# Half-height transposes and crossed projections in two places of four, with the rounding of silu's rows carried into the next step

## The chip, the cores and the metric

The kernel runs as one program on one core of a Trainium2 chip. The metric is the device time of one execution in microseconds, the median of several. Engines are named as in the profile: PE is TensorE's matmul, PEld its weight load, DVE is VectorE, ACT is ScalarE, POOL is GpSimd, SP is SyncE, which only issues DMAs here. SBUF is the on-chip memory with 128 partitions, PSUM the accumulator memory of eight banks into which PE writes.

## The reference

For each of 16 sequences of 512 rows and 256 columns, `x` is normalised to `xn`, and the result is `x + s * silu(ffn(xn))`. Two branches are computed from `xn`:

```python
# branch one: s, attention with a kernel over positions, then a feed-forward block
v = xn @ v_w + v_b                                     # 16 heads of 16
kern = einsum(weights of the 8 best of 16, sum of sines)   # one value per distance, per head
causal_kern = 3 * step(kern) * window
scores = causal_kern[i - j] + qm[i] + km[j] + 0.15 * (qc @ kc.T) / sqrt(8)
attn = softmax(where(i >= j, scores, -1e9))
h = layernorm(xn + (attn @ v) @ out_w + out_b)
s = layernorm(h + gelu(h @ ffn_w1 + b1) @ ffn_w2 + b2)

# branch two: a gated block whose inputs and weights are rounded to FP4 in blocks of 16 columns
def fp4_quant_dequant(x):
    scale = maximum(max(abs(block)) / 6, 1e-12)
    return nearest of (0, .5, 1, 1.5, 2, 3, 4, 6) to abs(x / scale), * sign * scale
hid = silu(q(xn) @ q(w_gate).T) * (q(xn) @ q(w_up).T)  # 704 columns
g = silu(q(hid) @ q(w_down).T)
out = x + s * g
```

All matrices are float32.

## The kernel before

The program keeps all weights in SBUF and goes through the 16 batches in order, each in four steps, here called places 0 to 3. A step works on four attention heads over all 512 rows, and at the same time on 128 rows of branch two (place t handles rows 128t to 128t+127). Work of three batches overlaps: while the heads of batch b are computed, the output, layer norm and feed-forward of batch b-1 (`old`) run in the same steps, and the projection of batch b+1 or b+2 is prepared. PE, DVE and ACT execute their instructions in exactly the order in which the main loop (lines 1149 to 1256) writes them; POOL and SP too run in program order.

One step runs so:

1. `context` (line 514): the products `cp` of the previous step's attention weights with the values, accumulated in one PSUM bank of its own, `cp`. `kept` (528) copies it to SBUF as `ct`, with columns reversed.
2. Five bursts of scores. Each burst has a `ws` group on PE, its Exp on ACT (`weights`, 478) and a multiplication by a table of the position kernel on POOL (`tabled`, L512 in the profile), and an `ms` group on PE, which computes scores of the next step for their row maxima, taken by DVE (`junk`, `mx`; `maxima`, 439).
3. Between the bursts other work is placed by the strings of `PLAN` (748), one for each place: `W` a `ws` burst, `M` an `ms` burst, `!` the maxima of what was found, and other letters one piece of a generator: `c` a piece of the next projection (`project`, 309), `l` a piece of the old batch's attention output (`output`, 550), `f` a piece of the old feed-forward's second product (`contract`), `x` the transposes of the rounded input of branch two (`turned_x`, 678), `y` those of silu's rounded rows (`turned_hidden`, 720, tiles `hqtp`), `h` those of the normalised rows, `k` a `kept` held back.
4. `hidden` (692): gate and up products of branch two in two halves of 352 columns. The first half goes to two ring banks (`gp`, `up`), the second to a pair of banks shared with the scores (`gu`). Between the halves PE turns the maxima (`mp`).
5. `gate` (730): the down product `dp` of the rows of the previous step, from the transposes of step 3.
6. In places 1 and 2, `expand` (616): the first product of the old batch's feed-forward with its Gelu, half of the rows in each. Places 0 and 3 have pieces of projections here.
7. The rounding of this step's 704 columns, `fp4_stages` (196): DVE takes the maximum of each block (`amax`) and its inverse, POOL multiplies by it (L222). Two DVE tensor_scalar passes make `m`, a power of two from the exponent bits times a constant; adding `m` and subtracting it rounds. POOL multiplies by the block's scale (L232). `ROUNDING` (670) gives the add and the subtraction to DVE, except in place 3, where POOL subtracts (L231). All of it is written before the next step begins.

`output` handles two row tiles of 128 at a time. For each, four groups of heads are transposed (`ctp`), divided by their softmax sums on DVE (`rinv`, `cx`), transposed back (`ct2`, shown as `ct<-ident,cx`), copied by ACT (`cT`), and multiplied by `wo` on top of a bias product (`op`). A helper `by_halves` (293) already does some transposes in halves of 64 rows, which go to the two banks of one pair: place 2 and 3's `xqtp` and one `htp`.

PSUM holds a pair used by `ws` and the second half of `hidden`, the bank of `cp`, and a ring of five banks for all else. Input rows `x` of batch b+2 are loaded and normalised at place 3 of batch b, and transposed (`xtp`) in place 0 of the next; the rounded input of branch two for rows 256 to 511 of a batch is made in its own place 1.

Quoted: the places' plans before.

```python
PLAN = ("WMc!llWM!xWM!ccllyWMlyW!M!l", "WMll!kWM!lWM!xllyhWMccy!WM!l",
        "WM!fffxM!fWffM!ffhM!ffWffM!fWfffWyy", "WM!fffxM!fWffM!ffWfM!ffWffM!fWffyy")
```

Of the kernel before, what the change touches and what calls it, by code (L numbers as in the profile page):

```python
# [13 lines left out]
I32 = mybir.dt.int32  # L14
# [30 lines left out]
LEVEL = 6291456.0  # L45
EXPONENT = 0x7F800000
# [4 lines left out]
def tile_block(ctx: ExitStack, tc: tile.TileContext, a: dict, pos: bass.AP, win: bass.AP, out: bass.AP):  # L51
# [45 lines left out]
    ps_c = ctx.enter_context(tc.tile_pool(name="ps_c", bufs=1, space=PSUM))  # L97
    ps = ctx.enter_context(tc.tile_pool(name="ps", bufs=5, space=PSUM))
# [95 lines left out]
    v_aug = [keep.tile([P, NT, H, VS], F32, name=f"va{i}", tag=f"va{i}") for i in range(2)]  # L194

    def fp4_stages(dst, src, n, width, engines=(dve, dve)):
# [26 lines left out]
        nc.gpsimd.tensor_scalar(scale, amax, 1.0 / 6.0, 1e-12, ALU.mult, ALU.max)  # L223
        yield
        m = sb.tile([P, I_FF], F32, name="m", tag="m")[:n, :width]
        dve.tensor_scalar(m.bitcast(I32), dst.bitcast(I32), EXPONENT, None, ALU.bitwise_and)
        dve.tensor_scalar(m, m, 1.0, LEVEL, ALU.max, ALU.mult)
        yield
        engines[0].tensor_tensor(dst, dst, m, ALU.add)
        yield  # L230
        engines[1].tensor_tensor(dst, dst, m, ALU.subtract)  # L231
        nc.gpsimd.tensor_tensor(blocks(dst), blocks(dst), per_block(scale), ALU.mult)  # L232

    def fp4(dst, src, n, width):
        for _ in fp4_stages(dst, src, n, width):
            pass
# [19 lines left out]
    mask = sb.tile([P, S], F32, name="mask", tag="mask")  # L256
# [14 lines left out]
    cp = ps_c.tile([P, S], F32, name="cp", tag="cp")  # L271
# [21 lines left out]
    def by_halves(name, dst, blocks):  # L293

        acc = ps_s.tile([P, 2, S], F32, name=name, tag="ws")
        for i, src in enumerate(blocks):
            for upper in range(2):
                k = slice(64 * upper, 64 * upper + 64)
                turn(acc[:, upper, i * 64 : (i + 1) * 64], src[k, :], ident[k, k])
        n = len(blocks) * 64  # L300
        act.copy(
            dst.rearrange("p (i u t) -> p u i t", u=2, t=64), acc[:, :, :n].rearrange("p u (i t) -> p u i t", t=64)
        )
# [4 lines left out]

    def project(b, x):

        xns[b] = []
        for pair in range(2):
            xns[b].append(sb.tile([P, 2, D], F32, name=f"xn_{b}_{pair}", tag="xn", bufs=6))
            for t in (2 * pair, 2 * pair + 1):
                act.activation(
                    rows_of(xns[b], t), x[:, t, :D], AF.Identity, bias=nmr[b][:, t : t + 1], scale=rstd[b][:, t : t + 1]
                )
            yield 0.0
# [64 lines left out]
        acc = projected(wq, P)  # L383
        split(acc, *halves("q", "hT" if b > 1 else "lo"), True, MIX / math.sqrt(8.0), None, (content(qi, 0, 1), content(qi, 2, 3)))
        yield 1.71
        acc = projected(wk, P)
        split(acc, *halves("k", "lo"), False, 1.0, None, (content(ki, 0, 2), content(ki, 1, 3)))
        yield 1.71
# [12 lines left out]
        va = v_aug[b % 2]  # L401
        vas[b] = va
        for t in range(NT):
# [3 lines left out]
            act.copy(va[:, t, :, 0:HD], vp[:, :D].rearrange("p (h d) -> p h d", d=HD))  # L407
# [106 lines left out]
    def context(b, g, where):  # L514

        for j in range(NT):
            n = S - j * P
            for i in range(4):
                mm(
                    cp[SLOT * i : SLOT * i + VS, :n],  # L520
                    vas[b][:, j, 4 * g + i, :],
# [4 lines left out]
                )  # L526

    def kept(b, g):
# [21 lines left out]
    def output(b, h, cts, half, mv):  # L550

        cTs, ops = {}, []

        def normal(t):
            tp = bank(f"ctp_{b}_{t}").rearrange("p (h s) -> p h s", s=SLOT)
            for g in range(H // 4):
                turn(tp[:, 4 * g : 4 * g + 4, :].rearrange("p h s -> p (h s)"), cts[g][:, t * P : (t + 1) * P])
            rinv = sb.tile([P, H], F32, name=f"rinv_{b}_{t}", tag="rinv", bufs=2)
            dve.reciprocal(rinv, tp[:, :, HD])
            cx = sb.tile([P, H, HD], F32, name=f"cx_{b}_{t}", tag="cx", bufs=3)  # L560
            dve.tensor_tensor(cx, tp[:, :, 0:HD], rinv.unsqueeze(2).to_broadcast([P, H, HD]), ALU.mult)
            return cx.rearrange("p h d -> p (h d)")

        def turned(t, cx):
            t2 = bank(f"ct2_{b}_{t}")
            for c in range(NC):
                turn(t2[:, c * P : (c + 1) * P], cx[:, c * P : (c + 1) * P])
            cTs[t] = sb.tile([P, D], F32, name=f"cT_{b}_{t}", tag="cx", bufs=3)
            act.copy(cTs[t], t2[:, :D])

        def product(t):
            acc = bank(f"op_{b}_{t}")
            op = acc[:, :D]
            biased(acc, 0, 1)
            cT = cTs[t]
            for c in range(NC):
                mm(op, cT[:, c * P : (c + 1) * P], wo[:, c, :], start=False, stop=(c == NC - 1), skip_group_check=True)
            later.append(lambda: added(h, (t,), acc, mv))

        first, second = 2 * half, 2 * half + 1  # L580
        cx = normal(first)
        yield 0.43
        cx2 = normal(second)
        yield 0.43
        turned(first, cx)
        yield 0.21
        turned(second, cx2)
        yield 0.21
        product(first)
        yield 0.96  # L590
        product(second)
        yield 0.96
# [23 lines left out]
    def expand(b, half, hT):  # L616

        acts = []
        for f in range(NF):
# [4 lines left out]
            act.activation(acts[f], fp[:, : 2 * P], AF.Gelu, bias=fb1[:, f : f + 1])  # L624
        return acts
# [44 lines left out]
    ROUNDING = [[dve if e == "d" else nc.gpsimd for e in by] for by in ("dd", "dd", "dd", "dg")]  # L670

# [20 lines left out]
    def hidden(b, t, xqT):  # L692
# [3 lines left out]
        def halves():  # L696
            for s in range(2):
                cut = slice(s * HI, (s + 1) * HI)
                if s == 1:
# [18 lines left out]
        return hid, halves(), fp4_stages(hid[:, :I_FF], hid[:, :I_FF], P, I_FF, ROUNDING[t])  # L718
# [18 lines left out]
    def expect(function):  # L737
# [6 lines left out]
        ("dddr|crd|dcdypr|xcr|cydd", "prrppo"),  # L744
        ("r|px|rpp|p|yyr", "pp"),
        ("p|x||yytt|tt", ""),
    )
    PLAN = ("WMc!llWM!xWM!ccllyWMlyW!M!l", "WMll!kWM!lWM!xllyhWMccy!WM!l", "WM!fffxM!fWffM!ffhM!ffWffM!fWfffWyy", "WM!fffxM!fWffM!ffWfM!ffWffM!fWffyy")

    def keeping(b, g):  # L750
        kept(b, g)
        yield 0.0

    def turning_h(b, half):
        turned_hs[half] = turned_h(b, xns[b], half, half == 1)
        yield 0.43

# [21 lines left out]
    plain = sb.tile([1, 2, D], F32, name="plain", tag="plain")  # L779
# [3 lines left out]
    nc.scalar.dma_start(out=vb, in_=a["v_b"].rearrange("(c p) -> p c", p=P))  # L783
# [247 lines left out]
    for k in range(H // 2 + 2):  # L1031
# [20 lines left out]
        if k > 1:  # L1052
            i = k - 2
            row = 2 * M * (i % 4)
# [9 lines left out]
    dve.memset(cp, 0.0)  # L1064
# [43 lines left out]
    nc.sync.dma_start(out=wo, in_=a["out_w"].rearrange("(c p) n -> p c n", p=P))  # L1108
# [32 lines left out]
    waiting, hq, cts, turned_hs, acts, coming, mv = None, None, [], {}, {}, None, None  # L1141
    xqTs, hqTs = {}, {}
# [6 lines left out]
    for s in range(STEPS):  # L1149
# [5 lines left out]
        if waiting is not None:  # L1155
            context(*waiting)
            if g != 1 or not has_old:
                kept(*waiting[:2])
# [176 lines left out]
```

## Time and profile before

| what | us |
|---|---|
| median of three runs (1848.93, 1850.88, 1851.63) | 1850.88 |
| profiled execution, its own time | 1850.01 |
| its span in the profile | 1848.3 |
| one batch in the steady part, four steps (756.17 to 860.00) | 103.83 |
| PE busy in that batch | 102.01 |
| DVE, ACT, POOL busy in that batch | 87.39, 62.31, 78.08 |
| one product by the table on POOL, mean of 448 | 1.75 |

The profile is that of one execution. A group of instructions in it stands under the line that recorded it; most engines' instructions were recorded by one helper at L72, so groups are told apart by the names of their tiles, as `hqtp<-ident,wide`. In a list over time a row has its start, its length, the engine, the line, the operation, out<-in, the partitions by elements and how many instructions were joined (x7); brackets at the end give the engine's idle time ahead of the row and what ended it. In a list of windows each engine has its busy time in that stretch. The length of a PE row includes the pipeline's fill, so that the distance of two starts, not the length, is what a group costs on PE. An expression like `PEclk` 1.00 is the share of full clock that TensorE was granted.

### The profile page before, as it was taken

Reading aid. Unit: us, or ns where it says so; the run is one execution under the profiler, and the core shown is the slowest. Engines: PE = TensorE matmul, PEld = TensorE weight load, DVE = VectorE, ACT = ScalarE, POOL = GpSimd, SP = SyncE. Lnnn points to the kernel's source line nnn. Section 1 sums busy time; section 2 is a strip of 40 time slices with the busy share of each in tenths; the row PEclk is TensorE's granted clock in tenths of the full one; section 3 lists DMA queues with packets and bytes.
Section 4 is the critical chain, followed back from the end, with each engine's and each line's share of the span. In section 5 each row is a group of like instructions: output and inputs, shape, how many; then the busy total and the mean of one; then the engine's idle time right before and its main releaser. Section 6 shows DMA issues by size and latency. Waiting matters only on the chain.

```text
span 1848.3 us, 33981 instructions
## 1 busy us (share of the span) xinstructions
PE 1745.7 (94%) x11491; PEld 1247.9 (68%) x11491; DVE 1487.9 (81%) x3917; ACT 1068.6 (58%) x1823; POOL 1313.4 (71%) x1128
## 2 busy tenths in 40 slices
PE   5769799999999999999999999999999999999998
PEld 2235467676776767677776767677776767677677
DVE  4868688888888888788888878888888888888754
ACT  5644455656565565556565565556566665555553
POOL 5467576778687776778687776778677776778671
PEclk8869799999999999999999999999999999999999
DMA  6254142423334242323334242323334242323200
GB/s 202 88 161 128 62 145 82 137 62 103 110 98 129 62 136 82 119 74 108 111 98 129 62 134 84 110 82 105 114 96 121 69 135 86 92 88 94 66 22 12
DMA packets 127122, 184.82 MB, mean 100 GB/s; under 512 B 15315, under 2 KB 57749, under 8 KB 126949
## 3 DMA queue, kind: packets, MB, share of 16 engines
q1 hardware_dynamic: 122496, 181.25, 31.8%
q8 instruction: 91, 1.49, 0.3%
q10 hardware_dynamic: 4004, 0.98, 0.3%
q14 instruction: 83, 0.67, 0.1%
q0 software_dynamic: 448, 0.42, 0.1%
HBM read 136.45 MB, written 45.09 MB: 98 GB/s over the span
## 4 chain that ended last, share of the span: by engine, by line
PE 76%; DVE 11%; POOL 3%; issue 1%; ACT 0%; DVEq 0%; POOLq 0%
PE f L72 23%; PE dp L72 8%; PE gu L72 7%; PE cp L72 7%; DVE junk L72 5%; PE ws L72 4%; PE op L72 4%; PE gp L72 4%; PE up L72 4%; PE ms L72 4%; PE vp L72 3%; PE hqtp L72 2%; POOL pr L512 2%; DVE cx L72 1%; PE qk_wk L72 1%; PE qk_wq L72 1%
## 5 line engine op out<-in xcount | busy, mean ns | idle before, releaser
L512 POOL TENSOR_TENSOR pr<-pr,table 128x1024 f32<-128x1024 f32 (+2 forms) x448 | 767.8, 1748 | 73.7 <-ACT pr L72 72.9
L72 DVE CUSTOM_DVE_ANT_0 junk<-ms,mask 128x512 bf16<-128x512 f32 (+3 forms) x1024 | 502.0, 490 | 148.3 <-PE ms L72 69.1
L72 ACT ACTIVATE pr<-ws 128x1024 f32<-128x1024 f32 x320 | 328.4, 1026 | 131.3 <-PE ws L72 126.4
L72 PE MATMUL f<-w,act 64*128 64x256 f32 (+1 forms) x1984 | 282.2, 382 | 0.0
L72 ACT ACT_TABLE_LOAD x168 | 215.5, 1283 | 64.1 <-PE gp L72 48.6
L72 PE MATMUL f<-hT,w 128*128 128x256 f32 x1024 | 226.3, 379 | 0.0
L72 PEld LDWEIGHTS f<-hT,w 128*128 128x128 f32 x1024 | 194.5, 190 | 26.6 <-ACT hT L72 0.2
L72 PEld LDWEIGHTS f<-w,act 64*128 64x128 f32 (+1 forms) x1984 | 197.8, 186 | 13.7
L232 POOL TENSOR_TENSOR wide<-wide,scale 128x704 f32<-128x704 f32 (+1 forms) x71 | 96.6, 1360 | 145.7 <-DVE wide L72 144.4
L72 PE MATMUL ws<-qT,kT 38*128 38x512 f32 (+3 forms) x1024 | 170.6, 388 | 21.3 <-ACT pr L72 16.4
L72 PE MATMUL ms<-kT,qT 36*128 36x512 f32 (+3 forms) x1024 | 166.2, 356 | 11.4 <-DMA kT<-k_d 6.7
L72 PE MATMUL dp<-wdT,hqT 128*128 128x256 f32 x768 | 176.2, 379 | 0.0
L72 PEld LDWEIGHTS dp<-wdT,hqT 128*128 128x128 f32 x768 | 145.8, 190 | 31.4 <-issue 6.7
L72 ACT ACTIVATE act<-f,fb 128x256 f32<-128x256 f32 x256 | 118.2, 474 | 75.3 <-PE f L72 72.4
L72 PE MATMUL cp<-pr,va 128*17 128x512 f32 (+3 forms) x2048 | 151.5, 434 | 0.0
L72 PEld LDWEIGHTS ws<-qT,kT 38*128 38x128 f32 x1024 | 90.4, 188 | 76.8 <-ACT pr L72 36.3
L223 POOL TENSOR_SCALAR scale<-amax 128x32 f32<-128x32 f32 (+1 forms) x104 | 39.2, 376 | 116.0 <-DVE amax L72 112.9
L72 PEld LDWEIGHTS cp<-pr,va 128*17 128x17 f32 x2048 | 54.3, 97 | 99.4 <-issue 75.3
L72 PEld LDWEIGHTS ms<-kT,qT 36*128 36x128 f32 x1024 | 104.7, 190 | 21.4 <-issue 14.4
L72 DVE TENSOR_TENSOR wide<-wide,m 128x704 f32<-128x704 f32 (+2 forms) x126 | 112.1, 889 | 4.1
L222 POOL TENSOR_TENSOR wide<-wide,inv 128x704 f32<-128x704 f32 (+1 forms) x71 | 99.1, 1396 | 21.6 <-DVE inv L72 21.1
L72 DVE SCALAR_TENSOR_TENSOR xn<-xn,rs,b 128x256 f32<-128x256 f32 x124 | 79.8, 643 | 35.9 <-POOL rs L114 30.7
(217 smaller groups left out, 3109.7 us busy)
## 6 DMA issues: line engine op xcount, KB each, us to landing
table<-rv SPq DMA_DIRECT2D x64, 1024.0 KB
kT<-k_d SPq DMA_DIRECT2D x256, 76.0 KB
qT<-q_d SPq DMA_DIRECT2D x256, 72.0 KB
x<-in_L_attn_x_dram SPq DMA_DIRECT2D x21, 512.0 KB
q_d<-q_hi SPq DMA_DIRECT2D x32, 256.0 KB
q_d<-q_lo SPq DMA_DIRECT2D x32, 256.0 KB
k_d<-k_hi SPq DMA_DIRECT2D x32, 256.0 KB
k_d<-k_lo SPq DMA_DIRECT2D x32, 256.0 KB
```

The costliest lines, as they stand in the source:

```text
L72: return lambda *args, **kw: self.follow(op(*args, **kw))
L222: nc.gpsimd.tensor_tensor(blocks(dst), blocks(src), per_block(inv), ALU.mult)
L223: nc.gpsimd.tensor_scalar(scale, amax, 1.0 / 6.0, 1e-12, ALU.mult, ALU.max)
L232: nc.gpsimd.tensor_tensor(blocks(dst), blocks(dst), per_block(scale), ALU.mult)
L512: nc.gpsimd.tensor_tensor(part, part, table[:, mine, j * P :], ALU.mult)
```

## The change

- `output` makes its transposes in halves of 64 rows, in two banks: eight half transposes for two row tiles in each direction. The products with `wo` run as pairs of 64-row matmuls, with one bias of half height for both tiles, and are joined by the existing `added_halves`.
- `project` computes q and k, and two of the four value tiles, by `crossed`: matmuls of 64 rows that go to two banks in turns, the second phase with the halves exchanged. It runs inside the bursts of places 0 and 1; its input is transposed in place 3, a step earlier (letter `i`), with the load of `x` at place 2, `xn` in seven buffers, and the small products `qk_m` at the end of place 0.
- `cp` comes from the ring, now of six banks, with a stationary of 32 columns in place of 17.
- The rounding of silu's rows and of branch two's input: ACT's Abs times 2^22 writes `m` in bfloat16, and two DVE scalar_tensor_tensor operations take `max(m, 1.25 * 2^22)` and add and subtract it. Weights keep the old way. Place 3's subtraction returns to DVE.
- The rounding of places 3 and 0 is carried into the next step: letter `a` does Abs or the add, `z` the rest with POOL's scaling. That of places 1 and 2 runs inside `expand`.
- In places 0 and 1 `hidden` takes the pair of score banks for its first half, and the transposes `hqtp` come behind the turned maxima, between the two halves. The transposes `xqtp` are in halves there too.
- The rounded input of rows 256 to 511 of a batch is made in place 3 of the batch before.
- Rows of `wo` and `v_b` are loaded in another order to suit the halves.

```diff
-        engines[0].tensor_tensor(dst, dst, m, ALU.add)
-        yield
-        engines[1].tensor_tensor(dst, dst, m, ALU.subtract)
+        if by_act:
+            nc.gpsimd.tensor_scalar(scale, amax, -1.0 / 6.0, -1e-12, ALU.mult, ALU.min)
+            yield
+            m = sb.tile([P, I_FF], BF16, name="m", tag="m")[:n, :width]
+            act.activation(m, dst, AF.Abs, scale=POWER)
+            yield
+            dve.scalar_tensor_tensor(dst, m, 1.25 * POWER, dst, ALU.max, ALU.add)
+            yield
+            dve.scalar_tensor_tensor(dst, m, 1.25 * POWER, dst, ALU.max, ALU.subtract)
...
         nc.gpsimd.tensor_tensor(blocks(dst), blocks(dst), per_block(scale), ALU.mult)
...
+    def crossed(acc, stationary, moving):
+        for phase, c in itertools.product(range(2), range(NC)):
+            for i in range(2):
+                k = slice(64 * i, 64 * i + 64)
+                of = i ^ phase
+                mm(
+                    acc[of], stationary(of, k, c), moving(of, k, c),
+                    start=(phase == 0 and c == 0), stop=(phase == 1 and c == NC - 1), skip_group_check=True,
+                )
+            yield phase, c
...
     def output(b, h, cts, half, mv):
+        tiles = (2 * half, 2 * half + 1)
+        acc = [bank(f"ctp_{b}_{half}_{upper}") for upper in range(2)]
+        for i, (t, g) in enumerate(itertools.product(tiles, range(H // 4))):
+            for upper in range(2):
+                k = slice(64 * upper, 64 * upper + 64)
+                turn(acc[upper][:, 64 * i : 64 * (i + 1)], cts[g][k, t * P : (t + 1) * P], ident[k, k])
...
+        acc = [bank(f"op_{b}_{half}_{upper}") for upper in range(2)]
+        biased(acc[0], 0, 2, 64)
...
-                if s == 1:
+                if s == in_pair:
                     both = ps_s.tile([P, 2, S], F32, name=f"gu_{b}_{t}", tag="ws")
...
     PLAN = (
+        "WM!lM!xWacclWM!llWcM!WcMz!ll",
+        "WM!lkxM!WacclWM!llWccM!WllMz!h",
+        "WM!fffxM!fWffM!ffhM!ffWffM!fWfffWyy",
+        "WM!fffxM!fWiffM!ffWfM!iffWffM!fWffyy",
+    )
...
-        pair, more = {1: (b, 2), 2: (b + 1, 0)}.get(g), iter(())
+        pair, more = {1: (b, 2) if b == 0 else None, 2: (b + 1, 0), 3: (b + 1, 2)}.get(g), iter(())
...
-        hq, halves, stages = hidden(b, g, xqTs.pop((b, g)))
+        hq, halves, stages = hidden(b, g, xqTs.pop((b, g)), 0 if has_old and g < 2 else 1)
         before = (b, g)
         ops = ahead
         next(halves)
         if following:
             subtracted(*following, ahead)
+        if has_old and g < 2:
+            for _ in hand["y"]:
+                pass
         next(norms, None)
         next(norms, None)
         next(halves)
         next(stages)
...
-            acts[g - 1] = expand(old, g - 1, turned_hs[g - 1])
+            acts[g - 1] = expand(old, g - 1, turned_hs[g - 1], stages)
...
-        for _ in stages:
-            pass
+        if has_old and g % 3:
+            for _ in stages:
+                pass
```

## The prediction

> **What bounds the kernel now.** I read the totals of the page first, then the busy time of each engine over one batch cut at its four steps, then the timelines of POOL and PE inside a step. Totals:
>
> ```profile
> PE 1745.7 (94%) x11491; PEld 1247.9 (68%) x11491; DVE 1487.9 (81%) x3917; ACT 1068.6 (58%) x1823; POOL 1313.4 (71%) x1128
> ```
>
> PE is busy 94%, but that average hides where it is not. The busy times of one batch, cut where each `cp` begins (columns: window, its length, PE, PEld, DVE, ACT, POOL, granted clock, DMA share, GB/s):
>
> ```profile
> 756.17:780.20 24.03, 22.76 (x141) 14.72 (x140) 19.53 (x58) 14.64 (x24) 18.40 (x14) 1.00 0.37 118
> 780.20:808.72 28.52, 27.97 (x180) 20.39 (x179) 25.21 (x68) 17.88 (x31) 19.29 (x15) 1.00 0.50 152
> 808.72:836.67 27.95, 27.95 (x210) 22.25 (x209) 23.92 (x58) 16.52 (x26) 21.25 (x19) 1.00 0.18 50
> 836.67:860.00 23.33, 23.33 (x181) 17.75 (x181) 18.73 (x52) 13.28 (x21) 19.14 (x16) 1.00 0.26 85
> sum 103.83, PE 102.01 PEld 75.10 DVE 87.39 ACT 62.31 POOL 78.08; mean PE 25.50 PEld 18.78 DVE 21.85 ACT 15.58 POOL 19.52
> ```
>
> Places 2 and 3 are PE from end to end; places 0 and 1, which the change rewrites, have PE idle 1.27 and 0.55 us. So PE sets each step, and a step gets shorter only if no other engine's chain becomes its length. The nearest other chain is POOL's. The POOL timeline of the steps of place 0 and place 1:
>
> ```profile
> 760.51 1.39 POOL L232 TENSOR_TENSOR wide<-wide,scale 128x704 f32<-128x704 f32 x1
> 761.86 11.94 POOL L512 TENSOR_TENSOR pr<-pr,table 128x1024 f32<-128x1024 f32 x7
> ...
> 783.05 1.39 POOL L232 TENSOR_TENSOR wide<-wide,scale 128x704 f32<-128x704 f32 x1 [3.12 <-DVE wide L72]
> 784.39 12.12 POOL L512 TENSOR_TENSOR pr<-pr,table 128x1024 f32<-128x1024 f32 x7
> ```
>
> Seven multiplications by the table run back to back for 12 us. The last scaling of silu's rows (1.39) runs before them, and what follows, `cp`, comes at 780.20 and 808.72, 6.4 and 12.2 us after the blocks end (773.80, 796.51): today the block is no limit. PE in the step of place 1:
>
> ```profile
> 782.48 0.51 PE L72 MATMUL ws<-qT,kT 38*128 38x512 f32 x2
> ...
> 788.84 0.60 PE L72 MATMUL hqtp<-ident,wide 128*128 128x128 f32 x4
> ...
> 794.29 1.35 PE L72 MATMUL gp<-wgT,xqT 128*128 128x352 f32 x4
> ...
> 796.66 0.27 PE L72 MATMUL mp<-ident,mx 128*16 128x128 f32 x1
> ...
> 799.13 2.75 PE L72 MATMUL dp<-wdT,hqT 128*128 128x256 f32 x12
> 801.72 7.07 PE L72 MATMUL f<-hT,w 128*128 128x256 f32 x32
> ```
>
> `hqtp`, which reads the scaled rows, is at 6.4 us after the first `ws`; then gate, up, `dp`, expand and the next `cp` follow with no gap.
>
> **The change, part by part.** All numbers are for a batch from the second on, times within a step from its first `ws`.
>
> *Less on PE.* In halves of 64 rows a transpose is cheaper: the rows with 64 partitions show 8 in 0.215 us, against 0.109 each for the full ones. Twelve `ctp`/`ct2`/`xqtp` transposes a step of places 0 and 1 give 1.5 us a batch; two joined biases instead of four (0.22 each to the next start) 0.6; fewer changes between 64 and 128 rows (0.11 each, 12 to 16 fewer) 1.3 to 1.8; the projection (3.43 for q and k), the value tiles (0.86) and the products stay as long, since a pair of 64-row matmuls takes 0.436 and two passes of a full one 0.43. With 1.8 us of stalls gone PE could be 4 to 5 us a batch shorter, all in places 0 and 1. The transposes of x move to place 3 (0.93), which gives a value tile (0.96) to place 1. Places 2 and 3 stay at 27.95 and 23.3.
>
> *Rounding.* Two DVE passes (0.53 each at the row `m<-wide`, more where POOL is in the way) become one Abs on ACT. No row has an Abs of 704 elements; the ACT rows of 512 (copy 0.59) and 1024 (Exp 1.03) bound it, and I take 0.75. DVE falls by about 8 us a batch, ACT rises by 4 to 66: both stay below PE, so the sums give nothing and cost nothing. The two other passes become scalar_tensor_tensor with a maximum. Not shown at 704; the row of the same shape without the scalar, 0.91, is its price unheld. Place 3's subtraction leaves POOL (1.69) for DVE.
>
> *The late scaling: where it goes wrong.* Rows of places 3 and 0 are now rounded inside the next step's weights. In the program order of POOL the scaling of these rows comes behind the seven table products, and PE's `hqtp` waits for it. `hqtp` is moved behind `mp`, and everything after it on PE, gp and up, `dp`, expand or `qk_m`, and the next `cp`, is queued behind that wait. So POOL's chain becomes the step.
>
> Place 1: the first Exp ends at 1.58 (0.55 from `ws` to Exp, as 782.48 to 783.02, then 1.03); the block from 1.65 to about 13.7; scaling 1.39: 15.1. Behind it `hqtp` 0.71, gp and up 2.37, `dp` 2.60, expand 7.0, `cp` 2.28: 14.96. Sum 30.05, against 28.52: +1.53. PE itself would be there at 12 to 13 (gp starts at 11.8 today; less `hqtp` 0.76, stalls 0.5 and about 1 of halves; plus gate and up of the first half 2.37 and `mp` 0.11; up to 1 more for waits on the maxima in DVE).
>
> Place 0: the ct copy stands before the first Exp, which ends at 1.65; the third weights come about 0.4 late behind Abs and cT copies on ACT; block to 14.03, scaling to 15.4; `hqtp` 0.71, gp and up 2.37, `dp` 2.68, `qk_m` 0.57, `cp` 2.28: 8.61. Sum 24.0, as now. POOL alone: +1.5 a batch.
>
> *DVE and POOL in each other's way.* Two rounding passes with two inputs in SBUF now fall inside the block of place 0 and of place 1. The profile shows what such an operation does beside POOL's:
>
> ```profile
> 828.54 1.28 DVE L72 SCALAR_TENSOR_TENSOR xn<-xn,mv,g 128x256 f32<-128x256 f32 x1
> ...
> 828.30 1.23 POOL L222 TENSOR_TENSOR xq<-xn,inv 128x512 f32<-128x512 f32 x1
> 829.50 0.90 POOL L663 TENSOR_TENSOR gated<-gated,xn 128x256 f32<-128x256 f32 x1
> ...
> 831.23 0.73 POOL L663 TENSOR_TENSOR gated<-gated,xn 128x256 f32<-128x256 f32 x1
> ```
>
> The DVE operation, 0.46 when alone, ends at 829.82, 0.29 after POOL's operation (829.53): it has waited for it. The next POOL operation then takes 0.90 in place of 0.73. For 704 elements the part behind POOL's end is 0.28 x 704/256 = 0.77, less the 0.11 that POOL gets back: 0.66 for each pass, 1.3 a step, 2.7 a batch, all on the chain just made critical. Bounds: 0 (they find POOL between two operations) and 0.91 each, 3.6 a batch. I take 2.7.
>
> [...]
>
> *The clock.* PE now idles 2 to 4 us in one piece in places 0 and 1. What idling does to the clock (columns as above):
>
> ```profile
> 1719.50:1723.08 3.58, 0.00 (x1) 0.03 (x1) 3.44 (x7) 0.84 (x1) 0.58 (x1) 1.00 0.00 0
> 1723.79:1730.62 6.83, 6.79 (x27) 5.12 (x27) 4.25 (x16) 2.73 (x5) 6.83 (x5) 0.50 0.00 1
> ```
>
> After 3.58 us without PE the granted clock is 0.50 for 6.8 us. A shorter dip is in the profile too: the step of place 1 that begins at 1091.72 has 3.4 us of half clock in the middle and takes 30.04, not 28.52: 1.5 a dip. Five of the 15 such steps have it. Bounds: none, and one in each of the two steps, 3.0 a batch. A gap of 2 to 4 us against a row of 3.58 is nearer to the full end, so 2.2 a batch, less the 0.5 that these steps lose today: +1.7.
>
> [...]
>
> *The rest.* `cp` takes a ring bank and 32 columns, at the same streaming length: nothing, since `cp`'s predecessor in the bank is several products old. ct's copy and the loads of x (issued at place 2, from SP, behind which only loads of scores queue; DMA share 0.18 there) are hidden; if the cover were gone, a load of x would be late by its landing, some 2 us, once a batch. Three more DMAs at the start lie beside the loading of weights, 0 to 1 us. Without a ready batch, start and first batch: DVE has fewer passes, PE more halves: -2, bounds -6 and +2. End: -1.
>
> *Sum.* 1.5 + 2.7 + 1.7 = 5.9 a batch, 15 batches, 88; less 3 for both ends: +85. The profiled execution took 1850.01 (span 1848.3), 0.9 under the median 1850.88, so the sum needs no correction: 1850 + 85 = 1935.
>
> **Rivals.**
> A: only the late scaling costs; the passes slip between POOL's operations and the clock holds. 15 x 1.5 - 3 = +20: 1870. For it: the block's length has hardly varied (11.94, 12.12); against it: the held rows.
> B: scaling and contention, no more half clock: 15 x 4.2 - 3 = +60: 1910. For it: gaps under 3.58.
> C, the other side: `hqtp` isn't late, and PE's savings show. This needs the scaled rows by 12.7 in place 1 (13.6 is the point at which that step is as long as before) and 13.4 in place 0; POOL's 12 us of products and 1.39 would have to be 2 us shorter or the block to start before the first Exp has ended. Then place 1 is 12.65 + 14.95 = 27.6 and place 0 22.0: -2.9 a batch, 1850 - 15 x 2.9 = 1806. Durations on POOL speak against it.
> D: worse. Abs, at 0.75, stands before an Exp and leaves POOL without work for that long in both steps: another 1.5 a batch: 1958.
> E: halves are no cheaper than full transposes (the change does not do what it says on PE). As POOL sets the step it moves little: as my forecast.
>
> **From cases to numbers.** Forecast with E 0.42, B 0.22, A 0.18, D 0.08, C 0.10. Of C I give 0.02 to a time within 0.2% of before (which is what a measurement here can tell from no change) and 0.08 to faster. The forecast's own range is 1915 to 1955. The range of 8 in 10 leaves out C and the upper half of D: 1864 to 1956.
>
> **What would show it.** Right: in places 0 and 1 POOL's scaling follows the seven products, PE idles before `hqtp` with POOL as releaser for 2 us or more, steps of 24 to 26.5 and 30 to 32.5, blocks of 13 us or more in place of 12, granted clock under 1.00 in them, DVE near 80 a batch and ACT near 66. Places 2 and 3 unchanged. Wrong: `hqtp` starts without a wait, place 1 under 28.5, or the block still ends by 12; then the step that failed is the POOL order or its block's start.

## The result: 10% slower, twice the loss that was forecast

The changed kernel takes 2037.43 us (median of 2034.19 to 2041.93) against 1850.12 for the kernel before, a ratio of 1.101 with a 95% interval of 1.099 to 1.104. The forecast was 1935, 1864 to 1956: the sign was right, and the time lies 81 us above the range. The profiled execution took 2034.19, its span is 2032.5.

The totals of the page of the changed kernel:

```profile
PE 1773.7 (87%) x12383; PEld 1286.4 (63%) x12383; DVE 1408.6 (69%) x3736; ACT 1123.9 (55%) x1921; POOL 1341.5 (66%) x1112
```

PE's share falls from 94% to 87%, though its busy time is 28 us longer: there are waits, and time at half clock. Where they are, the busy times of one batch show, cut at each `cp` as for the kernel before (window, length, PE, PEld, DVE, ACT, POOL, granted clock, DMA share, GB/s):

```profile
708.31:733.51 25.20, 21.88 (x178) 14.01 (x180) 20.37 (x55) 13.75 (x22) 18.83 (x13) 1.00 0.49 152
733.51:773.21 39.70, 31.23 (x205) 23.84 (x197) 21.16 (x61) 19.33 (x34) 19.55 (x14) 0.83 0.26 78
773.21:801.08 27.87, 27.87 (x209) 21.94 (x208) 21.99 (x55) 17.50 (x28) 22.05 (x19) 1.00 0.19 56
801.08:824.32 23.24, 23.24 (x185) 17.89 (x184) 19.27 (x55) 15.26 (x25) 20.19 (x18) 1.00 0.27 92
sum 116.01, PE 104.22 PEld 77.68 DVE 82.80 ACT 65.83 POOL 80.62; mean PE 26.06 PEld 19.42 DVE 20.70 ACT 16.46 POOL 20.16
```

Places 2 and 3 are as before (27.87, 23.24), place 0 is 1.2 longer, at 25.20. Place 1 takes 39.70 in place of 28.52, with a mean clock of 0.83: there lie 11.2 of the 12.2 us that this batch is longer. Over the batches place 1 takes 37.9 to 41.2 (the last batch apart), and place 0 takes 25.2 or 26.9. PE in that step (start, length, work, idle time ahead and what ended it):

```profile
735.78 0.49 PE L73 MATMUL ws<-qT,kT 38*128 38x512 f32 x2
...
742.56 0.76 PE L73 MATMUL ms<-kT,qT 36*128 36x512 f32 x1 [4.55 <-DMA kT<-k_d]
...
755.89 0.28 PE L73 MATMUL mp<-ident,mx 128*16 128x128 f32 x1 [2.12 <-DVE mx L73]
757.59 1.54 PE L73 MATMUL hqtp<-ident,wide 128*128 128x128 f32 x6 [1.42 <-POOL wide L242]
758.92 2.55 PE L73 MATMUL gp<-wgT,xqT 128*128 128x352 f32 x4
```

The wait for POOL ahead of `hqtp` is there, as forecast. But it is not the largest. In the second burst `ms` waits 4.55 us for a DMA, a load of `kT`; the forecast doesn't name that wait. (`qT` and `kT` are the operands of the scores in SBUF; the projected q and k lie in `q_d` and `k_d` in between, and are stored there from the tiles `q_hi`, `q_lo`, `k_hi`, `k_lo` and `ml`.) What precedes this load on its queue (SP's issues from place 0 on):

```profile
719.34 0.32 SPq L466 DMA_DIRECT2D qT<-q_d  x1
719.71 0.25 SPq L467 DMA_DIRECT2D kT<-k_d  x1
...
721.00 1.22 SPq L378 DMA_DIRECT2D q_d<-q_hi  x2
722.32 1.36 SPq L378 DMA_DIRECT2D k_d<-k_hi  x2
726.16 1.16 SPq L378 DMA_DIRECT2D q_d<-q_lo  x2
727.42 1.20 SPq L378 DMA_DIRECT2D k_d<-k_lo  x2
...
731.71 0.36 SPq L466 DMA_DIRECT2D qT<-q_d  x1
732.12 0.25 SPq L467 DMA_DIRECT2D kT<-k_d  x1
734.80 1.72 SPq L393 DMA_DIRECT2D q_d<-ml  x4
736.62 1.76 SPq L393 DMA_DIRECT2D k_d<-ml  x4
738.42 0.39 SPq L466 DMA_DIRECT2D qT<-q_d  x1
738.86 0.25 SPq L467 DMA_DIRECT2D kT<-k_d  x1
```

Place 1 needs eight loads of scores operands. Two pairs are issued at 719 to 720, the first after 6.8 us of waiting for a `ws` of PE; the third and fourth pair stand behind the stores of the next batch's q and k. (In the source all eight loads are written behind these stores: the order that counts is the one that SP was given when the program was built.) The stores of `q_lo` wait for DVE, which makes it at 725.44, and the stores of `ml` for the small products `qk_m`, which the change puts at the end of place 0. So the last load is issued at 738.86, 19.5 us after the first, and PE has its data at 742.56. In the batch of the kernel before that was cut into steps above, the eight loads go out from 767.90 to 774.87, and the stores of q and k from 776.62 on:

```profile
767.90 0.32 SPq L418 DMA_DIRECT2D qT<-q_d  x1
...
774.87 0.42 SPq L419 DMA_DIRECT2D kT<-k_d  x1
776.62 1.22 SPq L350 DMA_DIRECT2D q_d<-q_hi  x2
```

### The profile page after: what moved, and what is told of

Same layout as the page of the kernel before. It is cut to its first block, busy times and chain, and to the rows that moved or that the text cites. A ratio compares the mean times of both kernels' runs of the same rounds, so it can differ in the third digit from the quotient of the medians.

```text
span 2032.5 us, 35418 instructions
## 1 busy us (share of the span) xinstructions
PE 1773.7 (87%) x12383; PEld 1286.4 (63%) x12383; DVE 1408.6 (69%) x3736; ACT 1123.9 (55%) x1921; POOL 1341.5 (66%) x1112
## 4 chain that ended last, share of the span: by engine, by line
PE 64%; POOL 10%; DVE 6%; ACT 4%; issue 3%; DMA 3%; SPq 2%; POOLq 0%; DVEq 0%; ACTq 0%
PE f L73 22%; POOL pr L560 8%; PE dp L73 7%; PE cp L73 6%; PE gp L73 4%; PE up L73 4%; PE gu L73 4%; PE ws L73 3%; PE ms L73 3%; DMA kT<-k_d 3%; PE hqtp L73 3%; PE vp L73 2%; ACT pr L73 2%; DVE wide L73 2%; SPq L393 2%
## 5 line engine op out<-in xcount | busy, mean ns | idle before, releaser
L560 POOL TENSOR_TENSOR pr<-pr,table 128x1024 f32<-128x1024 f32 (+2 forms) x448 | 806.5, 1825 | 240.4 <-ACT pr L73 236.4
L73 PE MATMUL ms<-kT,qT 36*128 36x512 f32 (+3 forms) x1024 | 198.2, 393 | 86.4 <-DMA kT<-k_d 78.3
L73 ACT ACT_TABLE_LOAD x168 | 215.5, 1283 | 46.0 <-PE gu L73 27.4
L73 DVE SCALAR_TENSOR_TENSOR wide<-m,wide 128x704 f32<-128x704 bf16 x130 | 165.0, 1270 | 108.1 <-ACT m L73 105.9
L73 PEld LDWEIGHTS f<-hT,w 128*128 128x128 f32 x1024 | 194.5, 190 | 26.7 <-ACT hT L73 0.3
L73 PE MATMUL ws<-qT,kT 38*128 38x512 f32 (+3 forms) x1024 | 187.7, 406 | 20.7 <-ACT pr L73 9.0
L73 PEld LDWEIGHTS ms<-kT,qT 36*128 36x128 f32 x1024 | 116.6, 201 | 114.7 <-issue 80.2
L73 PE MATMUL cp<-pr,va 128*32 128x512 f32 (+3 forms) x2048 | 151.9, 435 | 0.0
L73 PEld LDWEIGHTS ws<-qT,kT 38*128 38x128 f32 x1024 | 102.2, 202 | 63.9 <-ACT pr L73 24.7
L222 POOL TENSOR_TENSOR wide<-wide,inv 128x704 f32<-128x704 f32 (+1 forms) x71 | 105.6, 1487 | 25.8 <-DVE inv L73 23.4
L73 PEld LDWEIGHTS cp<-pr,va 128*32 128x32 f32 x2048 | 62.1, 110 | 89.7 <-issue 69.4
L73 PE MATMUL gp<-wgT,xqT 128*128 128x352 f32 x256 | 109.2, 559 | 0.0
```

Of the source, the lines that this page charges most:

```text
L73: return lambda *args, **kw: self.follow(op(*args, **kw))
L222: nc.gpsimd.tensor_tensor(blocks(dst), blocks(src), per_block(inv), ALU.mult)
L560: nc.gpsimd.tensor_tensor(part, part, table[:, mine, j * P :], ALU.mult)
```

## The experiments

Steps are given as place 0 / place 1 in the steady part. Places 2 and 3 keep their 27.9 and 23.2 in all runs. The changed kernel has 25.2 / 39.7.

### Stores behind the loads

```diff
             def rest():
                 dve.scalar_tensor_tensor(lo[:, step], acc, by, hi[:, step].bitcast(F32), op, ALU.subtract)
-                for half, to in zip((hi, lo), places):
-                    for place in to:
-                        nc.sync.dma_start(out=place, in_=half.bitcast(F32))
+                def store():
+                    for half, to in zip((hi, lo), places):
+                        for place in to:
+                            behind_loads(nc.sync.dma_start(out=place, in_=half.bitcast(F32)))
+                stores.append(store)
...
             ahead = operands(*divmod(s + 2, H // 4))
+        caught_up(False)
```

The small parts of q and k (`ml`) likewise. In place 0 the stores that were put aside are issued by the last line; `behind_loads` orders each of them behind the last load of `operands`.

> The changed kernel, with one thing altered: in place 0 SP issues the stores of the next batch's q and k, and of their small parts, after the loads of scores operands of that step instead of between them. Theory S (the stores stand in SP's queue ahead of a load that place 1 needs, and the stall of 4.6 us on kT, with the half clock behind it, is most of the missing time): step of place 1 falls from 39.7 us to 31.4 to 33, no PE idle time with kT as releaser, 15 x about 7 = 105 us less, 1915 to 1945. Rival P (POOL's chain alone sets places 0 and 1, the late load lies beside it): place 1 stays over 37, time over 2000.

Measured: 1942.47 us, ratio 1.0498 (1.047 to 1.0525); 95 us less. The window of place 1 and the batch's sum:

```profile
922.62:955.67 33.05, 28.58 (x205) 21.22 (x197) 21.23 (x61) 19.16 (x34) 19.53 (x14) 0.95 0.38 117
...
sum 109.36, PE 101.56 PEld 75.02 DVE 82.83 ACT 65.68 POOL 80.59; mean PE 25.39 PEld 18.76 DVE 20.71 ACT 16.42 POOL 20.15
```

25.2 / 33.05 in most batches, and no wait for `kT` in the steady part. The last load of `kT` is issued at 910.81, the first store at 911.18. Half of the loss was the order of SP's queue. With it gone the kernel is at 1942, 7 us from the forecast of 1935, which had left these stores out. The rest of the forecast can now be read term by term, POOL first:

```profile
901.44 13.56 POOL L577 TENSOR_TENSOR pr<-pr,table 128x1024 f32<-128x1024 f32 x7 [0.63 <-ACT pr L73]
914.96 1.38 POOL L242 TENSOR_TENSOR wide<-wide,scale 128x704 f32<-128x704 f32 x1
...
926.54 13.37 POOL L577 TENSOR_TENSOR pr<-pr,table 128x1024 f32<-128x1024 f32 x7 [1.57 <-ACT pr L73]
939.87 1.39 POOL L242 TENSOR_TENSOR wide<-wide,scale 128x704 f32<-128x704 f32 x1
```

and PE of the same two steps:

```profile
914.70 0.28 PE L73 MATMUL mp<-ident,mx 128*16 128x128 f32 x1 [0.69 <-DVE mx L73]
916.40 0.87 PE L73 MATMUL hqtp<-ident,wide 128*128 128x128 f32 x6 [1.42 <-POOL wide L242]
...
939.61 0.28 PE L73 MATMUL mp<-ident,mx 128*16 128x128 f32 x1 [2.25 <-DVE mx L73]
941.31 0.98 PE L73 MATMUL hqtp<-ident,wide 128*128 128x128 f32 x6 [1.42 <-POOL wide L242]
942.08 2.55 PE L73 MATMUL gp<-wgT,xqT 128*128 128x352 f32 x4
944.43 1.81 PE L73 MATMUL up<-wuT,xqT 128*128 128x352 f32 x4
```

The first `ws` of these steps starts at 899.71 and 924.89, so `hqtp` starts at 16.7 and 16.4 us. The forecast's sums, 15.4 + 1.3 in place 0 and 15.1 + 1.3 in place 1, are 16.7 and 16.4. The last three products of the block show why it is longer (kernel with the stores behind the loads, then the kernel before):

```profile
908.89 6.11 POOL L577 TENSOR_TENSOR pr<-pr,table 128x768 f32<-128x768 f32 x3
```

```profile
769.00 4.80 POOL L512 TENSOR_TENSOR pr<-pr,table 128x768 f32<-128x768 f32 x3
```

6.11 against 4.80 is 1.31 more, for two DVE passes: 0.66 each, as worked out. And `gp`, 1.35 at full clock, takes 2.55.

### Rounding of places 3 and 0 in its own step

```diff
-        if has_old and g % 3:
+        if has_old:
             for _ in stages:
                 pass
```

> The changed kernel, with the rounding of places 3 and 0 finished in its own step, as before the change; the transposes hqtp stay late, SP's order of stores stays. Theory S: the late scaling is worth 2 to 4 us a batch, the late load of kT stays with all its price: 1975 to 2010, place 1 still 36 or more. Rival P (the late scaling is the whole cost): PE no longer waits for POOL in places 0 and 1, and the time is at or under 1850.

1978.55 us, ratio 1.0691 (1.0666 to 1.0716). That is 59 us less than the changed kernel. From the second batch on PE waits for POOL in hardly any step of places 0 and 1, the wait for `kT` is still there (4.3 to 5.9 us), place 1 is at 33.7 to 35.1, under the 36 that theory S gave it. POOL's late scaling alone was not the whole cost, as theory S had it. But place 0 got no shorter: 24.2 in some batches and over 27.5 in most.

### Both alterations

> Both alterations together: stores behind the loads, and rounding of places 3 and 0 in its own step. What is left of the change are the halves, the crossed projections, Abs on ACT and cp in the ring. Theory: no wait on POOL or kT in places 0 and 1, PE sets all four steps: 22 to 23.5, 27.6 to 28.5, 27.9, 23.3; 1805 to 1850. Rival D (DVE, whose two rounding passes stand between the steps again, delays the maxima and so the bursts): places 0 and 1 as long as before or longer, 1850 to 1890.

1952.17 us, ratio 1.0557 (1.0528 to 1.0585). My theory fell and rival D held: 10 us slower than with the stores alone, at 24.2 to 30.3 / 29.1 to 32.6. In place 0, on DVE, POOL and PE:

```profile
799.52 4.54 DVE L73 SCALAR_TENSOR_TENSOR wide<-m,wide 128x704 f32<-128x704 bf16 x2 [1.14 <-ACT m L73]
```

```profile
799.47 0.73 POOL L728 TENSOR_TENSOR gated<-gated,xr 128x256 f32<-128x256 f32 x1
800.97 2.35 POOL L577 TENSOR_TENSOR pr<-pr,table 128x1024 f32<-128x1024 f32 x1 [0.76 <-ACT pr L73]
```

```profile
804.72 1.22 PE L73 MATMUL qk_wq<-xnT,wq 64*128 64x512 f32 x1 [2.47 <-DVE mx L73]
```

The two rounding passes take 4.54 here: they end 0.74 after POOL's first table product (803.32). With POOL idle (from 767.49 to 773.87) they take 1.82, as in a place 1 of the changed kernel:

```profile
771.91 1.82 DVE L73 SCALAR_TENSOR_TENSOR wide<-m,wide 128x704 f32<-128x704 bf16 x2 [5.89 <-ACT m L73]
```

Behind them on DVE stand the first maxima, so PE stops for 2.47 us in the third burst and then has half the clock (0.83 over the step). What the two passes lose by waiting for POOL, 2.72 here (4.54 less 1.82), is more than the 1.31 that POOL lost to two passes with the stores behind the loads, and my forecast had counted only the latter.

### Scaling late, passes early

With the stores behind the loads, the rounding of places 3 and 0 in its own step, and POOL's last scaling ordered behind the seventh product (the three pieces are Abs and the two passes):

```diff
+            for _ in range(3):
+                next(stages)
...
+        if by_act and tables_done:
+            tc.add_manual_dep(last.ins, tables_done[-1].ins.name, in_order, reason="scale behind the tables")
```

> Stores behind the loads; Abs and the two DVE rounding passes of places 3 and 0 in their own step, but POOL's last scaling of those rows still held behind the seven table products of the next step. It tells the two terms of my forecast apart: against the first kernel of this call it has no DVE pass with two SBUF inputs beside the table products, against the third it has the late scaling. Forecast's terms: 2.7 us a batch less than the first (40 us) plus up to 1.7 a batch of clock, and 1.5 + 2.9 = 4.4 a batch (66 us) more than the third: 1870 to 1905. Rival (contention costs nothing): equal to the first within 10 us.

1972.65 us, ratio 1.0662 (1.0634 to 1.0691), outside what I expected: 25.3 to 29.3 / 32.3. It was meant to take the contention away, but only moved it to the head of the step, as in the run before. PE again stops up to 2.5 us for the first maxima in place 0. So it doesn't separate the two terms; what it shows is that the late scaling still costs on top (20 us over the kernel with both alterations).

### More passes in the block

```diff
     def completed(pieces):
+        for _ in range(2):
+            spare = sb.tile([P, S], BF16, name="spare", tag="junk")
+            dve.scalar_tensor_tensor(spare, wgT[:, 0, :S], 1.0, wuT[:, 0, :S], ALU.max, ALU.min)
         for _ in pieces:
```

> The kernel with the stores behind the loads, and two more DVE passes with two SBUF inputs (512 wide, result unused) put ahead of the two real ones inside POOL's block of places 0 and 1: the suspected cost doubled. By the forecast's rule each adds 0.28 x 512/256 - 0.11 = 0.45 us to POOL's block, 0.9 a step: blocks 13.5 to 14.4, steps 25.2 to 26.1 and 33.05 to 34, 15 x 1.8 = 27 us more than that kernel (1942): 1960 to 1980. Rival (DVE's passes cost POOL nothing, the block was long for another reason): blocks as before, time within 8 us of that kernel.

2036.05 us, ratio 1.1005 (1.0984 to 1.1026): 94 us more than the kernel with the stores alone, not 27; steps 30.0 / 35.0. On DVE, POOL and PE:

```profile
953.79 2.33 DVE L73 SCALAR_TENSOR_TENSOR spare<-wgT,wuT 128x512 bf16<-128x512 f32 x2
956.04 3.96 DVE L73 SCALAR_TENSOR_TENSOR wide<-m,wide 128x704 f32<-128x704 bf16 x2
```

```profile
952.62 5.71 POOL L577 TENSOR_TENSOR pr<-pr,table 128x768 f32<-128x768 f32 x3
```

```profile
961.91 0.38 PE L73 MATMUL mp<-ident,mx 128*16 128x128 f32 x1 [4.17 <-DVE mx L73]
```

POOL's last three products take 5.71, that is 0.91 more than in the kernel before, 0.45 for each added pass, as the forecast's sum has it. But the whole blocks, 13.16 and 12.98, are under the 13.5 to 14.4 that were expected, and under those without the added passes (13.56, 13.37). For the first real pass now meets the last product, the longest (2.35 in the kernel before), and waits for its end (958.33): it no longer lengthens the block. The maxima come late, and `mp`, not `hqtp`, sets the step. So in this run the price on POOL is as forecast for the passes that end before the block does (0.45 each), and the larger price is on DVE, which is the later of the two: its two real passes take 3.96, against 1.82 with POOL idle.

### Useless matmuls in the idle time

```diff
+    def filling(n):
+        acc = bank("filling")
+        for i in range(n):
+            mm(acc[:, : 2 * P], wgT[:, 0, :P], wgT[:, 0, : 2 * P], start=True, stop=True)
...
         next(halves)
+        if has_old and g == 1:
+            filling(10)
         if following:
             subtracted(*following, ahead)
         if has_old and g < 2:
+            filling(6)
             for _ in hand["y"]:
```

> The kernel with the stores behind the loads, and matmuls whose result nobody reads, put into PE's idle time: 10 (2.2 us) before the maxima are turned in place 1, 6 (1.3 us) before hqtp in places 0 and 1. If the idle time itself brings the half clock after it, the step of place 1 falls from 33.05 to 31.3 to 31.6 with the clock at 1.00 and place 0 stays at 25.2: 15 x 1.6 = 24 us less than that kernel, 1910 to 1925. Rival (the half clock has another cause, or the filling delays hqtp): 1942 or more.

1969.44 us, ratio 1.0641 (1.062 to 1.0663), 26.2 / 34.2, as the rival had it: I had the size wrong, since the trace has 20 instructions for the 10 of these matmuls (4.48 us) and 12 for the 6 (2.76 us), and the filling delayed `hqtp` by 2.9 us in place 1. From `hqtp` to the next `cp` it is 12.6 us, against 14.4 without filling. With half as many:

> As the kernel with the filling matmuls, but with half as many (each counted double there and delayed hqtp by 2.9 us in place 1 and 1 us in place 0; what followed hqtp still took 12.6 us at full clock, 14.4 without filling). If the idle time brings the half clock: place 1 at 31.3 to 31.7 in place of 33.05, place 0 at 25.2, 1910 to 1925, against 1942 with the stores behind the loads alone. Rival (the shorter tail came from something else): 1940 or more.

```profile
911.79:943.16 31.37, 30.37 (x221) 23.24 (x213) 21.15 (x61) 19.14 (x34) 19.52 (x14) 1.00 0.39 123
```

1911.47 us, ratio 1.033 (1.0313 to 1.0347), 25.2 / 31.37 at full clock: 31 us less than without the useless work. `hqtp` starts 16.4 us after the first `ws`, as without filling, and what follows is shorter: here the idle time itself brings the half clock (0.95 over the step without filling, 1.00 with it), at 1.7 us a batch in place 1. In place 0 it does so in some batches: without filling four of the first 14 such steps take 26.7 to 27.2, with it all 14 take 25.2. Both together are 2.1 us a batch (31 over 15).

### hqtp last

With the stores behind the loads (and behind the maxima): in places 0 and 1 the second half of gate and up before `mp`, and then, ahead of `hqtp` and `dp`, `qk_m` in place 0 and expand in place 1.

```diff
+        if has_old and g == 1:
+            acts[g - 1] = expand(old, g - 1, turned_hs[g - 1], stages)
+        if has_old and g < 2:
+            for _ in hand["y"]:
+                pass
         if gating:
             gate(*gating, hqTs.pop(gating))
```

> The kernel with the stores behind the loads (and behind the maxima), and hqtp later still: in places 0 and 1 gate and up of the second half come first, and in place 1 the whole of expand (7 us), in place 0 the small products qk_m; only then hqtp and dp. POOL's chain is then off the path. Theory: place 0 22.8 to 23.8, place 1 27.6 to 28.6, no half clock; 102 a batch against 104.3 of the kernel before: 1810 to 1840. Rival (the maxima on DVE, late by the held passes, hold mp and so the next ws): place 1 over 29.5, no faster than before.

1887.36 us, ratio 1.0199 (1.0172 to 1.0225), 23.7 / 31.3. Place 0 is as expected. Place 1 is as long as the rival had it, but not for its reason: `mp` comes without a wait, and the waits there moved on, to expand and `dp`:

```profile
922.87 3.72 PE L73 MATMUL f<-hT,w 128*128 128x256 f32 x16 [2.06 <-DVE wide L73]
...
928.39 2.86 PE L73 MATMUL dp<-wdT,hqT 128*128 128x256 f32 x12 [1.14 <-ACT hqT L73]
```

### hqtp inside expand, rounding of place 1 behind it

```diff
-            acts[g - 1] = expand(old, g - 1, turned_hs[g - 1], stages)
+            acts[g - 1] = expand(old, g - 1, turned_hs[g - 1], completed(hand["y"]))
+            for _ in stages:
+                pass
```

> As the kernel with hqtp last, with its two remaining stalls in place 1 taken away: hqtp stands in the middle of expand, where POOL's scaling is just done, and the rounding of place 1 follows expand, so that no Gelu is queued behind an Abs that waits for POOL; the first batch rounds in its own steps. Theory: place 1 from 31.3 to 28.0 to 28.8, place 0 23.7, 103 a batch, 1835 to 1850, at or a little under the kernel before (104.3 a batch). Rival (ACT's order or DVE's held passes keep place 1 over 30): 1860 or more.

1878.79 us, ratio 1.0149 (1.0133 to 1.0165), 23.7 / 29.7 to 31.6. The wait of `dp` is gone, that of expand is not. I had put it down to ACT, and it is the bank of `up`, which DVE releases only behind the layer norm (DVE, then PE):

```profile
914.32 0.52 DVE L73 TENSOR_TENSOR wide<-up,sl 128x352 f32<-128x352 f32 x1
```

```profile
914.89 2.07 PE L73 MATMUL f<-hT,w 128*128 128x256 f32 x4 [2.06 <-DVE wide L73]
```

With the first batch's rounding in its own steps, its place 3 falls from 45.7 to 41.4.

### The layer norm behind silu's second product

```diff
+        if has_old and g < 2:
+            next(halves)
+            if following:
+                subtracted(*following, ahead)
+            next(stages)
+            next(norms, None)
+            next(norms, None)
```

> As the kernel with hqtp inside expand, with one more order changed on DVE: in places 0 and 1 silu's second product, the maxima's low half and the block maxima come before the layer norm instead of behind it. There the bank of up, which expand needs for its fifth tile, was held until 914.8 by DVE, and PE stood 2.06 us and then had half the clock. Theory: place 1 from 29.7 to 31.6 to 27.8 to 28.4, place 0 23.7 or less, 103 a batch against 104.3 before: 1825 to 1848, the first version under the kernel before. Rival (another wait takes its place): 1855 or more.

```profile
873.68:901.06 27.38, 26.58 (x198) 20.25 (x197) 23.39 (x62) 20.26 (x34) 18.77 (x13) 1.00 0.46 144
...
952.18:975.84 23.66, 22.00 (x177) 13.95 (x176) 19.66 (x54) 13.95 (x23) 19.03 (x15) 1.00 0.42 130
sum 102.16, PE 99.69 PEld 74.06 DVE 83.99 ACT 66.99 POOL 80.06; mean PE 24.92 PEld 18.51 DVE 21.00 ACT 16.75 POOL 20.02
```

1828.18 us, ratio 0.9888 (0.9871 to 0.9904): faster than the kernel before by 1.1%, at 23.7 / 27.4 and full clock. All arithmetic of the change is still in it, halves, crossed projections, Abs and the rounding carried over; only the order of what waits is other (and the first batch rounds in its own steps). PE's work in the batch is 99.69, 2.3 less than before.

### Two counter-tests from there

SP's order as the change has it, put back:

```diff
-        holding[0] = has_old and g == 0
+        holding[0] = False
...
-            if first is not None:
+            if False:
                 tc.add_manual_dep(i.ins, first.ins.name, in_order, reason="loads first")
```

> The last kernel (1828, no wait on POOL and no half clock left), with SP's order as the change has it: the stores of q and k again between the loads of place 2's operands. If the late load alone has the price that the first experiment showed (95 us with the half clock behind it), place 1 goes from 27.4 to 32 to 35 with a stall on kT of 4 us or more, 15 x 4.6 to 7.5: 1897 to 1940. Rival (the load was late only because the rest of the step was late): within 15 us of 1828.

1927.61 us, ratio 1.0431 (1.0402 to 1.046), 23.7 / 34.1 to 34.8, with

```profile
930.81 0.76 PE L73 MATMUL ms<-kT,qT 36*128 36x512 f32 x1 [5.53 <-DMA kT<-k_d]
```

99 us for the order of the stores, in a kernel with no other wait of that size; the first experiment gave 95. And the rounding in its own step:

```diff
-        if g % 3 or not has_old:
+        if True:
             for _ in stages:
```

> The last kernel, with the rounding of places 3 and 0 finished in its own step: is carrying it into the next step a loss in itself? If DVE's two passes with two SBUF inputs then meet POOL at the head of the next step and the first maxima come 3 us late, as in the kernel with both alterations: place 0 at 26 to 29, place 1 at 29 to 31, 1870 to 1925. Rival (carrying was the loss): at or under 1828.

1943.95 us, ratio 1.0506 (1.0479 to 1.0533), at 29.4 to 31.2 / 28.4 to 30.7: the two passes take 4.54 us at the head of the step again, and PE stops 2.48 us. The time lies above the 1870 to 1925 that were expected, on the side away from the rival. In this kernel, with Abs on ACT, carrying the rounding over is no loss: without it the time is 116 us longer.

## Why the prediction was wrong, point by point

**The step that failed** is that on DMAs in "The rest": it prices the loads of x, "behind which only loads of scores queue", and three more DMAs at the start. (Its 2 us for the landing of x are an estimate; the one wait for x in the trace of the kernel before, DVE's at 5.36, is 2.52.) The change also moves the stores of q and k from the end of place 0 into its bursts, and `qk_m` from place 1 into place 0, and so their stores between the operand loads of place 2's scores. The forecast named SP only for x and set no price for the stores. That was worth 95 us (99 from the other side), about half of the 187 lost. The wait is 4.2 to 6.4 us a batch. It holds the second `ws`, so POOL's block and the scaling behind it; in the step that was shown `hqtp` starts 21.8 us after the first `ws`, not 16.4, and from there to the next `cp` it is 15.6 us, not 14.4, at half clock for longer (`up` takes 2.51 there, 1.81 with the stores behind the loads, 1.35 at full clock). That is the 6.6 us between 39.70 and 33.05.

**The late scaling** was right, in mechanism and size, once the stores are out of the way: POOL's scaling follows the seven products in both places, `hqtp` waits for it, and starts at 16.7 and 16.4 us, to a tenth what the forecast's chain and contention add up to.

**DVE beside POOL**: 0.66 on POOL for each pass of 704, and 0.45 for each of 512, both as worked out. Not seen was the other side: what the passes themselves lose. In most steps of the changed kernel it doesn't matter, since POOL is later (`mp` waits 0.7 and 2.1 for the maxima, `hqtp` 1.4 more for POOL). In five of the 15 steps of place 1 it does: there `mp` waits 3.6 for the maxima, and `hqtp` no longer for POOL. In the runs with the rounding in its own step, and in that with more passes, it decides.

**The clock**: 2.2 gross was the forecast, 1.7 net of the dips that the kernel before has already. The filled run took back 2.1 a batch, of which 1.7 in each step of place 1 and the rest in the four batches with a dip in place 0. (Of the kernel before, six of the 15 steps of place 1 have a dip, not five: 0.6 a batch, so 1.5 net.) The term was right in kind and near in size. With the stores behind the loads, two gaps of 2.25 and 1.42 with one `mp` of 0.28 between them brought the half clock in the step that was shown: the granted clock is 0.76 from 940.00 to 947.00. How long a gap must be, and whether gaps add up, isn't shown: with `hqtp` last, one gap of 2.06 ahead of expand left the clock of the step at 1.00 in 11 of 14 batches, and in the next run, with a gap of that length at the same place, it fell below 1.00 in nine of 14 (0.81 from 915.00 to 923.40 in the step shown).

**Start and end**: -3 was forecast, with bounds of -6 and +2 at the start. Up to place 0 of the second batch the changed kernel loses 8.1 us, outside these bounds, and from the last `cp` to the end of the span 4.3 more, where -1 stood. The first batch's place 3 went from 37.3 to 45.4, +8. There `hqtp` waits 4.6 us for POOL's scaling too. I had argued DVE's relief for that stretch, and not asked whether the late scaling holds there as well. Why the end is longer stays open.

**The sum**: 15 batches at 5.9 were 88. The kernel with the stores behind the loads is at 109.4 in most batches, against 103.8 before without a dip, 5.5 a batch; with the dips of both kernels, from place 0 of the second batch to the last `cp`, it loses 79 us, 5.2 a batch. Start and end add 5.9 and 4.8, where -3 stood for both. So the terms named for a batch hold nearly, and the omitted one explains the miss. That this kernel comes within 7 us of the forecast is partly luck: 9 too much in the batches and 14 too little at both ends nearly cancel.

**Rivals**: A and B are excluded by the 0.66 that each pass costs on POOL and by the filled run. E, halves no cheaper, is excluded too: sixteen half transposes of `ctp` take 0.54 to the next start (900.28 to 900.82, stores behind the loads), where eight full ones took 1.05 (759.10 to 760.15). C, the other side, was decided by the point named: with POOL's chain off the path, place 1 came to 27.4 and place 0 to 23.7, where 27.6 and 22.0 stood. PE is busy 22.00 in place 0; the other 1.7 are small waits that C had not. So PE's saving was overrated: 3.4 to 3.9 a batch of shorter work were forecast (4 to 5 with the stalls gone), and 2.3 of work and 1.7 of time were measured in the last kernel. D, Abs ahead of an Exp, isn't seen: Abs takes 0.78 (0.75 was estimated), and POOL's block in place 0 of the kernel with the stores behind the loads had gaps of 0.12 and 0.16 between its first three products only.

**Marks**: DVE fell to 82.8 a batch (near 80 said), ACT rose to 65.8 (66 said), places 2 and 3 did not move. Blocks of 13 us or more are there (13.56 and 13.37, stores behind the loads). The wait of `hqtp` with POOL as releaser is 1.42, not 2 or more, since PE first waits for the maxima; place 1, at 39.7 and at 33.05 with the stores behind the loads, is over the 30 to 32.5 that were named, place 0 is within 24 to 26.5 in most batches.

## What to carry to other kernels

When work is moved to another place, list its DMAs too, and read the whole order of the queue that issues them: here the stores of `q_lo` and `ml`, for which SP waited 2.4 and 2.6 us, held the loads behind them, the last to 738.86, and the loss showed in the next step, where PE waited 4.55 us for `kT`. If a block of an engine has no slack against the step, nothing that the critical engine waits for may stand behind it; put independent work, as expand here, between the block and its consumer. When one wait is taken away, look at once for the next one: here it took four of them until PE's savings showed: the load of `kT`, POOL's scaling, ACT's copy ahead of `dp`, and a PSUM bank that DVE's order held.

## What the runs showed of the hardware

DVE operations with two inputs in SBUF waited for the end of the POOL operation that they met: two passes of 704 took 4.54 us in the run with both alterations, where each met a POOL operation and the second ended 0.74 after POOL's, and 1.82 with POOL idle. POOL lost less: with the stores behind the loads its last three products grew by 1.31 for two such passes, 0.66 each. Useless work kept PE's clock up: 5 and 3 matmuls whose result nobody reads, in idle time, brought the step of place 1 from 0.95 to 1.00 of full clock and made the kernel 31 us faster (1942.47 to 1911.47), while 10 and 6 had 1.00 too, but delayed `hqtp` by 2.9 us in place 1 and made it slower (1969.44).
